# Reordering the steps of the first sweep in a two-sweep graph layer on one core

## The chip, the cores and the metric

One core of one Trainium2 chip runs the whole program. The metric is the device time of one execution in microseconds (us). Engines: PE is TensorE (PEld its weight loads), DVE is VectorE, ACT is ScalarE, POOL is GpSimd, SP is SyncE, which only issues transfers.

## The reference

64 samples of 256 tokens by 768 features. Per sample: layer norm and ReLU, then a graph layer with the adjacency matrix and its transpose, then a residual.

```python
h = jnp.maximum(_layernorm(x, axis=-1), 0.0)
ctx = jnp.matmul(adj, hs @ Wadj.T + badj) / deg_c[..., None]
ctx = ctx + jnp.matmul(radj, hs @ Wrev.T + brev) / rdeg_c[..., None]
ctx = ctx + hs @ Wself.T + bself
# ... plus two terms in the relations of the edges (rel), cut
x = x + ctx + rel
```

## The kernel before

Two sweeps over the samples: the first prepares features (three blocks per half: 0 and 1 in a tile `X`, 2 in a tile `Xs`), does some of the products and keeps `X` and `Xs` in HBM; the second loads them and does the rest. Nothing schedules the program but its own text: each engine runs its instructions in the order in which they are written. The text of a step is a list of items; primes say for how many samples ahead an item works (`xt''` in step t loads for sample t+2). Bare numbers such as `11a` or `2` are matrix products, with what ACT and DVE do for them. `d` holds four values per token (mean, scale and two degrees) in HBM, and `row` is the copy of it on every partition.

```python
for t in range(B):
    order = FIRST if t == 0 else SECOND if t == 1 else STEP1 if t + 1 < B else LAST1
    run(order, t, 1, PARTS1, PLACES1)
```

So STEP1 serves t = 2 to 62, 61 steps. The items that matter here:

```python
def store_left(b, n):                       # storeX, storeXs: issued on ACT
    ...
    nc.scalar.dma_start(s["kept_" + n], ...)          # X: 1536 KB, Xs: 768 KB

def spread(b):                              # spread
    nc.tensor.transpose(pt, v.rearrange("p c k -> p (c k)"), ident)   # one small transpose per step
    nc.scalar.activation(line, pt, AF.Copy)
    ...
        for c in range(C):                  # two pieces of 2 KB to HBM
            nc.sync.dma_start(d[:, c, :], line[c * 64 + NMEAN : c * 64 + RRDEG + 1, :])
        nc.sync.dma_start(                  # read back, one copy per partition: 512 KB
            s["row"].rearrange("p k i -> p (k i)"), d.rearrange("k c p -> (k c p)").partition_broadcast(P)
        )

# load_xt (xt): Xs <- x_t, 768 KB.  load_x (x): x, 768 KB.  load_sums (o0, o1), store_sums (out0, out1): 384 KB each.

def self_features(b, k):                    # self0, self1: on POOL, in place on Xs
    eng.tensor_tensor(v, v, row[:, k : k + 1, :].to_broadcast(...), op=(ALU.add, ALU.mult)[k])
def relu_features(b):                       # relu: on ACT
    nc.scalar.activation(S[b]["Xs"], S[b]["Xs"], AF.Relu)
def statistics(b, c):                       # on DVE, from x
    nc.vector.bn_stats(s["stats"][:, c, n, :], ...)
def aggregate(b, f):                        # u0 to u5: four matmuls into a bank pa (two of them), read by DVE
    ...
    nc.vector.tensor_mul(s["X"][:, f, :, :]..., pa, s["row"][:, 2:4, :]...)
```

## Time and profile before

| | us |
|---|---|
| timed executions, median of the first three | 2796.19 |
| the profiled execution, by itself | 2781.24 |
| its span | 2779.4 |
| of it: up to step 2 | 69.6 |
| steps 2 to 7 | 171.5 |
| steps 8 to 61 (54 steps) | 1389.4 |
| the rest, which is nearly all second sweep | 1148.9 |

A step is counted from one small transpose `pt` to the next. The main lines of this profile stand in the prediction below. POOL's order of time in one step (start, length, what): `self0'`, `a2+b2` and `self1'`. The first waits for the transposed x.

```profile
1101.80 3.52 POOL L534 TENSOR_TENSOR Xs<-Xs,row 128x1536 f32<-128x1536 f32 x1 [2.12 <-DMA Xs<-in_x_t_dram]
1105.27 1.85 POOL L562 TENSOR_TENSOR Xs<-Xs 128x768 f32<-128x768 f32 x1
1107.08 3.52 POOL L534 TENSOR_TENSOR Xs<-Xs,row 128x1536 f32<-128x1536 f32 x1
```

The transfer view of the stretch 1092.5 to 1094.4 us of the same step: per queue the packets, megabytes and share of the 16 engines. q10 is ACT's queue, q1 is SyncE's.

```profile
q10 hardware_dynamic: 112, 0.69, 88.6%
q1 hardware_dynamic: 8, 0.00, 0.5%
```

In these 1.9 us ACT's store of `Xs` has the engines nearly to itself. The 8 packets of SyncE's queue are the first piece of d and its completions; the second piece, issued at 1092.24, isn't among them.

### The profile page before, as it was taken

Reading aid. Unit: us, or ns where it says so; the run is one execution under the profiler, and the core shown is the slowest. Engines: PE = TensorE matmul, PEld = TensorE weight load, DVE = VectorE, ACT = ScalarE, POOL = GpSimd, SP = SyncE. Lnnn points to the kernel's source line nnn. Section 1 sums busy time; section 2 is a strip of 40 time slices with the busy share of each in tenths; the row PEclk is TensorE's granted clock in tenths of the full one; section 3 lists DMA queues with packets and bytes.
Section 4 is the critical chain, followed back from the end, with each engine's and each line's share of the span. In section 5 each row is a group of like instructions: output and inputs, shape, how many; then the busy total and the mean of one; then the engine's idle time right before and its main releaser. Section 6 shows DMA issues by size and latency. Waiting matters only on the chain.

```text
span 2779.4 us, 45451 instructions
## 1 busy us (share of the span) xinstructions
PE 2686.8 (97%) x16854; PEld 2472.1 (89%) x16854; DVE 2069.8 (74%) x3142; ACT 1757.2 (63%) x3099; POOL 1869.9 (67%) x1290
## 2 busy tenths in 40 slices
PE   5989999999999999999999998999999999999999
PEld 4779888888888898988898887899999999999998
DVE  7567776776777777777677775778888887887887
ACT  3557766766666766766676663566666656666665
POOL 5777777777777777777777775565565555555553
PEclk9999999999999999999999998999999999999999
DMA  7667777777777777777777777566666666766764
GB/s 251 250 222 262 260 256 254 256 260 258 255 262 252 263 263 258 266 255 262 252 259 260 260 249 253 211 243 252 256 243 247 257 247 241 259 245 241 258 248 162
DMA packets 237355, 695.46 MB, mean 250 GB/s; under 512 B 19388, under 2 KB 97716, under 8 KB 220744
## 3 DMA queue, kind: packets, MB, share of 16 engines
q1 hardware_dynamic: 200264, 390.49, 41.9%
q10 hardware_dynamic: 36864, 302.01, 27.4%
q8 instruction: 135, 2.21, 0.3%
q14 instruction: 92, 0.75, 0.1%
HBM read 436.05 MB, written 256.37 MB: 249 GB/s over the span
## 4 chain that ended last, share of the span: by engine, by line
PE 57%; DMA 15%; POOL 12%; DVE 7%; ACT 5%; issue 3%; SPq 1%; ACTq 0%; POOLq 0%; DVEq 0%
PE x L579 13%; DMA x<-in_x_dram 6%; POOL Xs L534 6%; DMA Xs<-in_x_t_dram 6%; PE y L579 5%; PE pa L545 4%; PE s L568 4%; PE z L579 4%; PE t L568 3%; PE u L568 3%; PE v L568 3%; PE x L568 3%; PE w L579 2%; PE s L579 2%; DMA d<-line 2%
## 5 line engine op out<-in xcount | busy, mean ns | idle before, releaser
L562 POOL TENSOR_TENSOR X<-X,Xs 128x768 f32<-128x768 f32 x256 | 475.9, 1881 | 464.5 <-DMA Xs<-kept_Xs 432.7
L534 POOL TENSOR_TENSOR Xs<-Xs,row 128x1536 f32<-128x1536 f32 (+1 forms) x128 | 446.8, 3491 | 215.7 <-DMA Xs<-in_x_t_dram 210.4
L294 ACT ACTIVATE top<-l 128x768 f32<-128x768 f32 x450 | 367.2, 816 | 219.4 <-DVE l L312 161.3
L312 DVE SCALAR_TENSOR_TENSOR l<-l,top 128x768 fp32r<-128x768 f32 x450 | 429.1, 954 | 15.4
L545 PE MATMUL pa<-a,hilo 128*128 128x512 f32 x1536 | 398.0, 400 | 37.3 <-DVE X L550 24.6
L545 PEld LDWEIGHTS pa<-a,hilo 128*128 128x128 f32 x1536 | 275.5, 189 | 101.6 <-DVE X L550 35.5
L579 PE MATMUL y<-w,X 128*128 128x256 f32 x1536 | 353.5, 380 | 0.0
L579 PEld LDWEIGHTS y<-w,X 128*128 128x128 f32 x1536 | 283.5, 190 | 34.4
L311 DVE TENSOR_TENSOR l<-X,top 128x768 fp32r<-128x768 f32 x285 | 269.9, 947 | 35.8 <-ACT top L294 35.1
L309 ACT ACTIVATE l<-X 128x768 fp32r<-128x768 f32 x285 | 238.0, 835 | 25.3 <-issue 19.1
L550 DVE TENSOR_TENSOR X<-pa,row 128x512 f32<-128x512 f32 x384 | 246.6, 681 | 9.0 <-PE pa L545 8.9
L423 DVE BATCH_NORM_STATS2 stats<-x 128x6 f32<-128x384 f32 x252 | 127.9, 549 | 149.9 <-DMA x<-in_x_dram 149.9
L562 POOL TENSOR_TENSOR a1+b<-X 128x768 f32<-128x768 f32 x64 | 118.1, 1845 | 155.1 <-PE w L579 154.4
L500 DVE SCALAR_TENSOR_TENSOR hilo<-x,cols,top_h 128x768 fp32r<-128x768 f32 x126 | 127.7, 1014 | 82.8 <-ACT top_h L294 82.8
L579 PE MATMUL x<-w,X 128*128 128x256 f32 x780 | 181.7, 383 | 1.2 <-issue 0.9
L579 PE MATMUL x<-w,Xs 128*128 128x256 f32 x768 | 176.2, 379 | 0.6 <-issue 0.6
L579 PE MATMUL w<-w,a1+b 128*128 128x256 f32 x768 | 176.4, 379 | 0.0
L579 PE MATMUL z<-w,Xs 128*128 128x256 f32 x768 | 176.1, 379 | 0.0
L579 PEld LDWEIGHTS x<-w,X 128*128 128x128 f32 x780 | 144.9, 192 | 19.0 <-issue 1.5
L579 PEld LDWEIGHTS x<-w,Xs 128*128 128x128 f32 x768 | 141.1, 190 | 18.0 <-issue 1.3
L579 PEld LDWEIGHTS z<-w,Xs 128*128 128x128 f32 x768 | 141.4, 190 | 16.8
L579 PEld LDWEIGHTS w<-w,a1+b 128*128 128x128 f32 x768 | 141.0, 190 | 16.7
(208 smaller groups left out, 6293.7 us busy)
## 6 DMA issues: line engine op xcount, KB each, us to landing
kept_X<-X ACTq DMA_DIRECT2D x64, 1536.0 KB
X<-kept_X ACTq DMA_DIRECT2D x64, 1536.0 KB
o<-in_x_dram SPq DMA_DIRECT2D x128, 384.0 KB
Xs<-in_x_t_dram SPq DMA_DIRECT2D x64, 768.0 KB
kept_Xs<-Xs ACTq DMA_DIRECT2D x64, 768.0 KB
sums<-o SPq DMA_DIRECT2D x128, 384.0 KB
o<-sums SPq DMA_DIRECT2D x128, 384.0 KB
Xs<-kept_Xs ACTq DMA_DIRECT2D x64, 768.0 KB
```

Of the source, the lines that this page charges most:

```text
L294: nc.scalar.activation(top.rearrange("p (f i) -> p f i", i=of.shape[-1]), of, AF.Copy)
L309: nc.scalar.activation(first, value, AF.Copy, scale=LOWER)
L311: nc.vector.tensor_tensor(others, value, top, op=ALU.subtract)
L312: nc.vector.scalar_tensor_tensor(diff, others.bitcast(F32), -STEP, top, op0=ALU.mult, op1=ALU.add)
L423: nc.vector.bn_stats(s["stats"][:, c, n, :], (s["o", c] if b == 0 else s["x"][:, c, :])[:, ts(n, HO)])
L500: nc.vector.scalar_tensor_tensor(hilo[:, 1, c, :], S[b]["x"][:, c, :], rstd, top, op0=ALU.mult, op1=ALU.subtract)
L534: eng.tensor_tensor(v, v, row[:, k : k + 1, :].to_broadcast([P, f1 - f0, L]), op=op)
L545: nc.tensor.matmul(pa, hilo[:, part, c, ts(f, P)], s["a"][:, c, :, :].rearrange("p s i -> p (s i)"), start=(k == 0), stop=(k == 2 * C - 1),)
L550: nc.vector.tensor_mul(s["X"][:, f, :, :].rearrange("p s i -> p (s i)"), pa, s["row"][:, 2:4, :].rearrange("p s i -> p (s i)"))
L562: (eng or nc.gpsimd).tensor_tensor(L[name], L[x], L[y], op=op)
L568: nc.tensor.matmul(bank, l[k][:, f, :], r[k][:, f, :], start=(k == 0 and f == 0), stop=(k == 1 and f == F - 1))
L579: nc.tensor.matmul(bank, l[:, f, :], r[:, f, :], start=(start and f == 0), stop=(row is None and f == F - 1), skip_group_check=not start,)
```

## The change

Its intent: STEP1 was ordered anew with a model of the transfers in which those in flight share the DMA engines equally. The same 52 items, permuted; nothing else.

```diff
 STEP1 = """
-self0' degrees0'' left' u4' u3' 5a statistics0'' 10a 5 u5' a2+b2 u0' self1' s11 statistics1'' degrees1'' 10
-u2' u1' s13 adj''' o1' 11a normal'' tokens'' 8 relu' 11 b0+b1' a0+a1+b0+b1 storeX' normalise1'' 2 s5' spread'' 3
-storeXs' normalise0'' a1+b1' xt'' second1'' b2-a1' second0'' 13a a1+b0+b1' x''' 14 13 s10' out1 out0 o0'
+left' a2+b2 u3' degrees0'' u4' 5a degrees1'' statistics0'' 10a adj''' self0' 5 u5' u0' s11 statistics1''
+self1' 10 u2' u1' s13 a0+a1+b0+b1 normal'' 11a tokens'' relu' 8 11 b0+b1' storeXs' normalise1'' storeX' o1'
+s5' 2 spread'' 3 normalise0'' second1'' second0'' 13a xt'' 14 x''' b2-a1' a1+b1' out1 13 a1+b0+b1' o0' out0
+s10'
 """
```

## The prediction

> **What bounds the kernel now.** I read the page first: the engines' shares, then the forty slices.
>
> ```profile
> PE 2686.8 (97%) x16854; PEld 2472.1 (89%) x16854; DVE 2069.8 (74%) x3142; ACT 1757.2 (63%) x3099; POOL 1869.9 (67%) x1290
> PE   5989999999999999999999998999999999999999
> DMA  7667777777777777777777777566666666766764
> ```
>
> TensorE (PE) is the bound; nothing else is near full. The second sweep begins near 1760 us. In the table by stretches its PE is busy 350.00 of 350 us (1850 to 2200) and 500.00 of 500 (2200 to 2700): nothing to gain there, and the change doesn't touch it. In the first sweep the same table has 296.15 of 300 (700 to 1000) and 292.68 of 300 (400 to 700). So all that this change can win is PE's idle time in the first sweep.
>
> Next, who waited for whom between 400 and 1600 us (about 47 steps; one step is one sample):
>
> ```profile
> POOL Xs L534 <- DMA Xs<-in_x_t_dram: 159.2, 47, 5.8
> DVE stats L423 <- DMA x<-in_x_dram: 120.9, 47, 4.7
> PEld pa L545 <- DVE X L550: 27.8, 35, 2.7
> PE pa L545 <- DVE X L550: 20.5, 27, 2.5
> ```
>
> PE's only wait of note is for a bank `pa` that VectorE (DVE) has not read yet; DVE was held before it by `statistics0''`, waiting for the load of x. GpSimd (POOL) waits longest, for the transposed x, but that has slack. A step with such a stall, on PE:
>
> ```profile
> 822.97 0.87 PE L579 MATMUL z<-w,l 128*128 128x256 f32 x6
> 825.38 2.13 PE L545 MATMUL pa<-a,hilo 128*128 128x512 f32 x8 [1.55 <-DVE X L550]
> ```
>
> I cut the sweep at the one small transpose per step (`pt`, L450) and measured 54 steps (about 241 to 1631 us). PE's own work is 25.08 us (1091.32 to 1116.40 is such a step, without a gap). The mean is 25.73, so 0.65 us of stall per step. All of it sits 15.94 us after `pt`, and its size follows one thing: when the statistics start. Up to 13.44 us after `pt` there is no stall, later each us costs a us (start 14.22: step 25.83; 15.31: 26.92; correlation 0.99). Mean start: 14.10. STEP1 is used for t = 2 to 62, 61 steps: 61 x 0.65 = **40 us, the most that the change can win**.
>
> Now why x comes late. The load queue of SyncE in that step without a gap:
>
> ```profile
> 1091.93 0.60 SPq L457 DMA_DIRECT2D d<-line  x2
> 1095.38 0.34 SPq L458 DMA_DIRECT2D row<-d  x1
> 1095.77 0.86 SPq L464 DMA_DIRECT2D kept_line<-line  x1
> 1096.73 0.38 SPq L389 DMA_DIRECT2D Xs<-in_x_t_dram  x1
> 1097.89 0.38 SPq L379 DMA_DIRECT2D x<-in_x_dram  x1
> 1098.33 1.75 SPq L402 DMA_DIRECT2D sums<-o  x2
> 1105.78 0.33 SPq L395 DMA_DIRECT2D o<-in_x_dram  x1
> ```
>
> `row` must wait until both 2 KB pieces of d have landed, 3.45 us after the first issue. By the packet records, the first piece moves 0.74 us after its issue, the second only 2.2 us after its own, just when the 768 KB of kept_Xs end. That store was issued on ScalarE (ACT) at the same moment:
>
> ```profile
> 1110.87 1.48 ACT L537 ACTIVATE Xs<-Xs 128x1536 f32<-128x1536 f32 x1
> 1112.01 0.33 ACTq L517 DMA_DIRECT2D kept_X<-X  x1
> 1117.01 0.31 ACT L462 ACTIVATE tokT<-line 128x128 fp32r<-128x128 f32 x1
> 1117.02 0.33 ACTq L517 DMA_DIRECT2D kept_Xs<-Xs  x1
> ```
>
> After that the SyncE queue runs as one train: row packets 1096.34 to 1098.79, transposed x to 1101.27, x after it. Over the 54 steps, row is issued 4.37 us after `pt` and the statistics start 9.73 us later (standard deviation 0.36). So **the issue of row sets the stall**.
>
> **What the Trainium skill says.** "DMA: Bandwidth & Descriptors", section Queues, rings and completion order: SP and ACT each have one ring on each of the 16 DMA engines, an engine takes descriptors of a ring in order and changes ring only after a whole packet of several descriptors. The trace agrees: kept_Xs gives each engine 8 descriptors (128 rows on 16), and the 2 KB piece sits behind all of them. In the second sweep, a 64 KB load issued at 2007.98, in the middle of the 1536 KB load of X (packets 2005.79 to 2010.67), moves its first packet at 2011.34. And within SyncE's ring, the 384 KB store issued 0.44 us behind the 768 KB load of x lets the next load go about 1.0 us after x arrives; with equal shares the half-sized one would be first. So the model behind this change, equal shares, isn't what this trace shows. The same page, section Issuing engines are not separate DMA queues, says that the starting engine gives no lane of its own: agrees. "Perfetto Trace Analysis", section Identifying the Most-Contended Engine, warns that matmul occupancy isn't distance from roofline; here it serves only to find gaps, and weight loads stand at 89%.
>
> **The change part by part.** The same 52 items, permuted; no instruction is added or removed. An engine runs its own items in order, so I compared the five orders.
>
> PE: u3' and u4' change places. Worth 0. SyncE: only o0' now goes before out0. o0' waits until out1 has landed (issue near 14.5 us after `pt`), so the 384 KB of out0 leave about 6.5 us later, behind x instead of close after it. Since it was behind x in the ring already: 0 to 0.1 us.
>
> POOL: a2+b2 (1.85 us) moves ahead of self0', into time in which POOL waits for the transposed x (2.12 us in the step shown); a0+a1+b0+b1 (1.83 us) moves ahead of normal''. From arrival to normal'' it was 3.52 + 1.85 + 3.52 = 8.9 us, it becomes 3.52 + 3.52 + 1.83 = 8.9 us. Worth 0; relu' could start 1.85 us earlier, but on ACT it stands behind 11a. DVE: s5' goes before 2, so it needn't wait for that product (2.0 us): b2-a1' comes some 1.5 us earlier, off the path. ACT: degrees1'' (1.8 us) moves between 5a and 10a; product 10 reads its bank near 15.1 us after `pt`, the scaling is then done by 13.7. Worth 0.
>
> The part that counts is ACT's stores: kept_Xs goes right behind relu', kept_X behind normalise1''. Counting from the next `pt`: relu' ends at -4.0 (1112.35 against 1116.40), kept_Xs is issued at -3.9, its packets start 0.85 later and take 2.1 (as they do now): -3.0 to -0.9. kept_X follows in the same ring, 3.9 to 4.3 us long as now: **-0.9 to about 3.0 to 3.4**. d is issued at about 0.6 as before and now meets the large store instead of the small one. It moves when that store has drained, about 3.0 to 3.4, and row goes out 0.64 us later, as now: 3.65 to 4.05, against a mean of 4.37. Gain on row, transposed x and x: 0.3 to 0.7, I take 0.45 us. Taking 0.45 off each of the 54 measured starts and keeping what lies above 13.44 leaves 0.33 us of stall instead of 0.68 on this measure: 0.35 x 61 = 21 us. Some of it I expect back from the stores' own scatter (kept_X lasts up to 5.2 us now), so I take 18: 2796 - 18 = **2778 us**.
>
> **The rivals.**
> 1. *Equal shares hold.* Then d slips past kept_X, row goes out near 2 us after `pt`, x is bound by its own issue (6.6), and the stall vanishes: 2796 - 40 = 2756. Against it: every one of the measured second pieces of d waited for the store's end.
> 2. *The large store holds d longer than the small one did.* Two stores back to back add their scatter; if kept_X drained at 4.3, row would go out at 4.95, 0.6 late: 1.26 - 0.68 = 0.59 us more per step, 36 us, 2832. For it: kept_X is twice as long, starts after its companion and depends on relu', hence on the transposed x. Against it: the sum above, which puts its end before the present one.
> 3. *A new wait.* a1+b0+b1' overwrites part of X and must wait for kept_X to land, now about 4 to 5 us after `pt`; POOL has until about 11 to start self0' and 3.7 us of work before it, so it should be absorbed. In the same way o1' now waits for out0 (about 18 us); it is needed a step later. About 2796 if this just eats the gain.
>
> **Range and chances.** 2756 needs the stall gone; 2800 is nothing gained. Runs before spread over 9 us. Range 2757 to 2806. Faster by 2% means 2740, below the floor of 2756: 0.01. Slower by 2% means 2852, 0.9 us more per step: 0.05. Rest 0.94.
>
> **What would show it.** Stall at the same place (pa after `pt`), smaller; statistics starting near 13.7 instead of 14.10; d's wait up to row shorter by some 0.4 us and both pieces of d moving when kept_X ends; POOL's wait for the transposed x about 2 us shorter per step through a2+b2 alone; second sweep unchanged. I am wrong if row goes out later than 4.4 after `pt`, or if PE shows a wait other than `pa`.

## The result

The changed kernel takes 2757.0 us (median of 4; 2749.22 to 2759.21) against 2797.48 us for the kernel before in the same rounds. The ratio is 0.9853, 95% interval 0.9822 to 0.9884. A ratio here is the mean time of one kernel's fast runs over that of the other's of the same rounds, so not quite the ratio of the two medians. The gain is 40 us. I had predicted 18, and the time lies on the lower edge of my range.

The page of the changed kernel: PE's, PEld's and the transfers' busy tenths.

```profile
PE   5989999999999999999999998899999999999999
PEld 4778999889899998989999997899999999999998
DMA  7676777777777777777777767576666666666764
```

Tenths are too coarse to show it; the table by stretches isn't. These are the lines of steps 8 to 61, first of the kernel before, then of the changed one (stretch, length, busy time of PE, PEld, DVE, ACT, POOL, then granted clock, DMA share and GB/s).

```profile
241.10:1630.50 1389.40, 1366.36 (x8048) 1233.01 (x8047) 1006.05 (x1674) 956.91 (x1782) 1060.90 (x811) 1.00 0.73 258
```

```profile
245.60:1607.00 1361.40, 1358.41 (x8048) 1232.52 (x8047) 1003.00 (x1675) 939.24 (x1783) 1068.59 (x810) 1.00 0.75 264
```

The same 8048 matmuls, and PE's idle time in this stretch falls from 23 to 3 us. (Busy time shrinks by 8 us too, in part because the record draws some matmuls behind a stall longer, as the 2.13 us for eight of them in the prediction's stall, where 2.02 is usual. The stretch itself is 28 us shorter; e1 below shows that this execution of the kernel before was a fast one.) The second sweep is the same: 350.00 of 350 and 500.00 of 500 us busy, as before.

Who waited for whom, 400 to 1600 us, in the changed kernel (total, times, longest):

```profile
POOL Xs L535 <- DMA Xs<-in_x_t_dram: 95.1, 48, 3.4
DVE stats L424 <- DMA x<-in_x_dram: 86.7, 48, 2.9
PEld pa L546 <- DVE X L551: 5.0, 10, 0.8
PE pa L546 <- DVE X L551: 2.8, 8, 0.6
```

PE's waits for a bank `pa` are down from 27.8 and 20.5 us to 5.0 and 2.8. They are the same waits at the same place, 15.95 us after `pt`, only rarer. The waits of POOL and DVE for loads shrink far less, and needn't: DVE has slack up to 13.44 us after `pt`.

ACT and SyncE in one step of the changed kernel (`pt` at 1455.94):

```profile
1450.41 1.48 ACT L538 ACTIVATE Xs<-Xs 128x1536 f32<-128x1536 f32 x1
1451.92 0.33 ACTq L518 DMA_DIRECT2D kept_Xs<-Xs  x1
1453.40 0.33 ACTq L518 DMA_DIRECT2D kept_X<-X  x1
```

```profile
1456.56 1.24 SPq L458 DMA_DIRECT2D d<-line  x2
1459.33 0.34 SPq L459 DMA_DIRECT2D row<-d  x1
1459.72 0.43 SPq L465 DMA_DIRECT2D kept_line<-line  x1
1460.24 0.38 SPq L390 DMA_DIRECT2D Xs<-in_x_t_dram  x1
1462.34 0.38 SPq L380 DMA_DIRECT2D x<-in_x_dram  x1
```

`kept_Xs` goes out right after the ReLU, `kept_X` 1.5 us later. By the packet records of this step, the packets of `kept_X` run from 1454.68 to 1458.53, and both pieces of d, issued at 1456.56 and later, move at 1458.38 to 1458.51. So d does wait until the store has all but drained, 1.8 us. That is still less than before, and row is issued 2.77 us after d instead of 3.45.

Means over steps 8 to 61, in us after `pt` unless said otherwise, with the standard deviation in brackets:

| | before | changed |
|---|---|---|
| kept_Xs issued | 0.85 | -4.02 (0.00) |
| kept_X issued | -4.34 | -2.45 (0.17) |
| last piece of d moves | 3.68 (0.36) | 2.74 (0.28) |
| row issued | 4.37 (0.39) | 3.60 (0.36) |
| transposed x has moved | 11.25 (0.77) | 10.37 (0.70) |
| statistics start | 14.10 (0.60) | 13.26 (0.54) |
| stall of PE per step | 0.65 | 0.13 |

### The profile page after: what moved, and what is told of

It is laid out like the page before. It is cut to its first block, busy times and chain, and to the rows that moved or that the text cites. A ratio compares the mean times of both kernels' runs of the same rounds, so it can differ in the third digit from the quotient of the medians.

```text
span 2757.4 us, 45566 instructions
## 1 busy us (share of the span) xinstructions
PE 2684.1 (97%) x16854; PEld 2476.0 (90%) x16854; DVE 2069.8 (75%) x3142; ACT 1737.5 (63%) x3099; POOL 1873.5 (68%) x1290
## 4 chain that ended last, share of the span: by engine, by line
PE 82%; DMA 7%; DVE 5%; POOL 3%; ACT 2%; issue 1%; SPq 0%; ACTq 0%; DVEq 0%; POOLq 0%
PE x L580 14%; PE y L580 11%; PE pa L546 10%; PE w L580 6%; PE z L580 6%; PE s L569 6%; DMA x<-in_x_dram 3%; PE t L569 3%; PE u L569 3%; PE v L569 3%; PE x L569 3%; PE s L580 3%; PE w L569 3%; PE z L569 2%; PE y L569 2%; PE v L580 2%
## 5 line engine op out<-in xcount | busy, mean ns | idle before, releaser
L563 POOL TENSOR_TENSOR b2-a<-Xs,X 128x768 f32<-128x768 f32 x64 | 118.9, 1857 | 185.3 <-DVE l L312 185.3
L312 DVE TENSOR_TENSOR l<-b0+b,top 128x768 fp32r<-128x768 f32 x62 | 59.2, 954 | 141.9 <-ACT top L295 141.9
```

Of the source, the lines that this page charges most:

```text
L312: nc.vector.tensor_tensor(others, value, top, op=ALU.subtract)
L563: (eng or nc.gpsimd).tensor_tensor(L[name], L[x], L[y], op=op)
```

## The experiments

**My theory** after the result: ACT's two stores alone decide, through d, row and x. **Rivals:** SyncE's exchange of `out0` and `o0'` (a store less beside x, which would matter with equal shares), and the moves on the other engines. Ratios are to the kernel before, in the same rounds on the same chip (e1 to e4 on one chip, e5 to e11 on another). Row, statistics and stall are means of steps 8 to 61 of one profiled execution each. All runs gave correct results.

| run | row issued | statistics start | stall per step | median us | ratio (95%) |
|---|---|---|---|---|---|
| e1, before again | 4.31 | 14.16 | 0.77 | 2795.85 | 0.9992 (0.9968 to 1.0015) |
| e2, stores only | 3.90 | 13.63 | 0.37 | 2770.5 | 0.9908 (0.9888 to 0.9928) |
| e3, all but stores | 4.41 | 14.08 | 0.71 | 2792.26 | 0.9979 (0.9958 to 1.0000) |
| e4, SyncE only | 4.41 | 14.11 | 0.75 | 2790.97 | 0.9975 (0.9951 to 0.9999) |
| e5, stores and POOL | 3.53 | 13.37 | 0.16 | 2760.28 | 0.9873 (0.9851 to 0.9895) |
| e6, transposed x ahead of row | 3.59 | 12.57 | 0.03 | 2754.91 | 0.9851 (0.9826 to 0.9876) |
| e7, kept_X ahead of relu' | 3.47 | 13.36 | 0.40 | 2773.3 | 0.9917 (0.9882 to 0.9953) |
| e8, kept_Xs late | 2.53 | 14.30 | 0.88 | 2801.76 | 1.0025 (0.9991 to 1.0058) |
| e9, both behind relu' | 3.30 | 13.19 | 0.16 | 2762.46 | 0.9867 (0.9835 to 0.9899) |
| e10, changed again | 3.61 | 13.43 | 0.22 | 2762.92 | 0.9878 (0.9854 to 0.9902) |
| e11, e6 again | 3.55 | 12.68 | 0.05 | 2754.92 | 0.9849 (0.9826 to 0.9873) |

### e1: the kernel before, once more

No edit.

> The kernel before, unchanged, profiled once more. My prediction took the stall (0.65 us per step, 40 us in all) from one execution of 2781 us, while the timed ones lie near 2797. Theory: the timed executions lose the missing 16 us to the same stall, so a profiled execution near 2797 shows about 56 / 61 = 0.9 us of stall per step, at the same place (the bank pa), the statistics starting near 14.35 us after pt, and the second sweep as long as before. Rival: the 16 us lie elsewhere (second sweep, clock, start), and the stall per step stays 0.65 at whatever time. Ratio to the kernel before 1.000 within 0.004 either way.

The profiled execution took 2797.01 us. Its line for steps 8 to 61:

```profile
252.10:1648.10 1396.00, 1369.27 (x8049) 1235.51 (x8048) 1006.86 (x1674) 957.46 (x1783) 1062.37 (x811) 1.00 0.73 257
```

So 0.77 us of stall per step, more than the 0.65 of the first record but less than the 0.9 expected. Against the first record, this stretch is 6.6 us longer, steps 2 to 7 are 8.2 us longer (179.7 against 171.5), the start 2.8 longer and the rest 1.9 shorter. The theory is half right: my base execution was a lucky one, some of its luck lay in the stall, and as much in the first steps. From this execution to the changed kernel's, 37.7 us go: 34.6 in steps 8 to 61, 4.7 in steps 2 to 7, 1.8 at the start, and 3.4 come back in the rest. Steps 2 to 7 take 171 to 180 us in all runs, whatever the order (171.5 in the first record, 171.0 in e2, 179.4 in e3, 171.1 in e10). The granted clock of that stretch goes along with it: 0.98 or 1.00 in the records with 171 to 172 us, 0.95 to 0.97 in all those with more. Which is cause and which effect isn't settled here.

### e2 and e3: the stores alone, and all but the stores

```diff
 # e2, on the kernel before
-... relu' 11 b0+b1' a0+a1+b0+b1 storeX' normalise1'' 2 s5' spread'' 3 storeXs' normalise0'' ...
+... relu' storeXs' 11 b0+b1' a0+a1+b0+b1 normalise1'' storeX' 2 s5' spread'' 3 normalise0'' ...
 # e3, on the changed kernel
-... b0+b1' storeXs' normalise1'' storeX' o1' s5' 2 spread'' 3 normalise0'' ...
+... b0+b1' storeX' normalise1'' o1' s5' 2 spread'' 3 storeXs' normalise0'' ...
```

> The kernel before with nothing changed but the two stores of ScalarE: kept_Xs right behind relu', kept_X behind normalise1''. Theory (the stores hold up d, d holds up row, row holds up x): row is issued near 3.6 us after pt instead of 4.37, statistics start near 13.3, stall near 0.13 us per step, ratio 0.985 to 0.988, so the whole gain. Rival 1 (the gain comes from SyncE's exchange of out0 and o0', which takes a store out from behind x): ratio 0.995 to 1.000 and the statistics near 14. Rival 2 (ScalarE's, VectorE's and GpSimd's other moves): the same, 0.995 to 1.000.

> The changed kernel with the two stores of ScalarE put back where the kernel before has them. Theory: the gain is gone, ratio 0.996 to 1.002, row issued near 4.3 us after pt, stall 0.6 us per step or more. Rivals 1 and 2: ratio near 0.985 to 0.990, because the exchange on SyncE and all other moves are kept.

e3 came out as the theory has it: without the stores' move hardly anything is left (0.9979). But e2 missed the 0.985 to 0.988 that I expected: it brings only 26 of 40 us, so the stores alone aren't the whole. Two parts that give 26 and 6 us apart give 40 together: something else helps the stores. The table of e2 shows where: `kept_Xs` is issued at -3.65 us with a scatter of 0.35, in the changed kernel at -4.02 with none. The view of the tile Xs in e2 (241 to 1600 us; idle us, times) says what held up the instructions that use it; the second line is the ReLU waiting for POOL (a third, 2.3 us for the adjacency load, is left out).

```profile
  DMA Xs<-in_x_t_dram: 156.0, 53
  POOL Xs L534: 13.9, 25
```

### e4: SyncE's exchange alone

```diff
-... s10' out1 out0 o0'
+... s10' out1 o0' out0
```

> The kernel before with only o0' and out0 exchanged on SyncE. Theory: x is ahead of out0 in the same ring anyway, so statistics start no earlier than 14.0 us after pt, ratio 0.997 to 1.002. Rival 1 (equal shares between transfers in flight, so 384 KB less beside x): x arrives up to 1 us earlier, the statistics start near 13.4, ratio 0.985 to 0.990.

The statistics start 14.11 us after `pt`, 9.70 after row's issue; in the two records of the kernel before it was 9.73 and 9.85. So x isn't faster with one store less behind it, and rival 1 falls. The ratio of 0.9975 lies within the 0.997 to 1.002 that the theory expected, and its interval nearly touches 1; steps 8 to 61 are as long as e1's within 1.3 us (1394.7). If there are 7 us in it, they aren't in the stall that this study is about. That is left open.

### e5: the stores and POOL's exchange

```diff
 # on e2
-self0' degrees0'' left' u4' u3' ... 5 u5' a2+b2 u0' self1' ... 11a normal'' ... b0+b1' a0+a1+b0+b1 normalise1'' ...
+left' a2+b2 self0' degrees0'' u4' u3' ... 5 u5' u0' self1' ... 11a a0+a1+b0+b1 normal'' ... b0+b1' normalise1'' ...
```

> The kernel before with the stores moved as in e2 and, on GpSimd, a2+b2 ahead of self0' and a0+a1+b0+b1 ahead of normal''. e2 alone gave 0.991, because kept_Xs went out at -3.65 us before pt with a scatter of 0.35, while in the changed kernel it goes out at -4.02 with none. Theory: relu' (and so kept_Xs) waits for self1', which the transposed x holds up; with a2+b2 out from between self0' and self1' that wait is gone. Then kept_Xs is issued at -4.0 with a scatter under 0.1, row near 3.6, stall near 0.15 us per step, ratio 0.984 to 0.987: the whole gain of the change. Rival: GpSimd's exchange is worth nothing, as I predicted (the chain up to normal'' has the same length), and the rest of the gain comes from the other moves: ratio near 0.991, kept_Xs at -3.65 as in e2.

`kept_Xs` is issued at -4.02 with no scatter, the stall is 0.16 and the time 2760.28 us. The same view of the tile Xs as for e2 has one line left:

```profile
  DMA Xs<-in_x_t_dram: 42.8, 43
```

The ReLU never waits for POOL now: `a2+b2` is out from between `self0'` and `self1'`, so when the transposed x comes late, `self1'` ends 1.85 us sooner. The ratios of e2 and e5 alone would be thin evidence, since their intervals just overlap; the scatter of `kept_Xs` and the view above carry the argument. GpSimd's two exchanges weren't tried apart. Together with the stores they are the change, as far as can be measured. The others (PE's, DVE's, ACT's degrees, SyncE's, and on GpSimd `b2-a1'` going before `a1+b1'`) account for what is between 0.9873 and the 0.9853 and 0.9878 of the changed kernel, which is nothing that can be told from noise.

### e8: the small store out of d's way, but late

```diff
 # on the kernel before
-... spread'' 3 storeXs' normalise0'' a1+b1' xt'' second1'' b2-a1' second0'' 13a ...
+... spread'' 3 normalise0'' a1+b1' xt'' second1'' b2-a1' second0'' storeXs' 13a ...
```

> The kernel before with kept_Xs moved late instead of early: behind second0'', when d and row are long issued. Theory (the second piece of d is held by kept_Xs alone): both pieces move 0.75 us after their issues, row is issued near 2.4 us after pt instead of 4.3. But kept_Xs then moves beside the transposed x and x, 768 KB or 1.9 us at 400 GB/s, so the statistics start between 12.4 and 14.2 us after pt and the ratio lies between 0.98 and 1.00. Rival (d is slow by itself, not because of the store): row stays near 4.3.

SyncE in one step:

```profile
1054.35 0.61 SPq L457 DMA_DIRECT2D d<-line  x2
1055.94 0.34 SPq L458 DMA_DIRECT2D row<-d  x1
1056.33 0.43 SPq L464 DMA_DIRECT2D kept_line<-line  x1
1056.87 0.38 SPq L389 DMA_DIRECT2D Xs<-in_x_t_dram  x1
```

row follows d by 1.59 us instead of 3.45, on average it is issued at 2.53: the store was what made d wait longer than this. Yet the kernel isn't faster: the statistics (14.30) and the ratio (1.0025) lie just outside what I expected. `kept_Xs`, issued at 4.77, now moves from 8.17 to 11.96 on average, among the packets of the transposed x and x. Row is 1.8 us earlier than in e1, and the statistics start 0.1 later. The whole gain at one end of the train is lost in its middle.

### e7 and e9: does the order of the two stores matter?

```diff
 # both on the changed kernel
-... tokens'' relu' 8 11 b0+b1' storeXs' normalise1'' storeX' o1' ...
+... tokens'' storeX' relu' storeXs' 8 11 b0+b1' normalise1'' o1' ...       # e7
+... tokens'' relu' storeX' storeXs' 8 11 b0+b1' normalise1'' o1' ...       # e9
```

> The changed kernel with kept_X issued ahead of relu' and kept_Xs behind it: both stores early, in the other order. Theory (d waits until ScalarE's ring is drained, whatever is last in it): the ring drains at the same time or up to 0.3 us earlier, row at 3.2 to 3.7 us after pt, ratio 0.984 to 0.987 as for the changed kernel. Rival (it matters that the small store is out of the way and the large one last): row near 4.3 and ratio near 0.995.

> The changed kernel with both stores right behind relu', the large one first: relu' storeX' storeXs'. It does properly what e7 set out to do: e7 held relu' behind the large store's wait, so line and d came 1.0 us late (d issued at 1.62 us after pt). Theory (d waits until all of ScalarE's ring is drained; the order within it doesn't matter): kept_X goes out near -4.4, kept_Xs near -4.0, the ring drains near 2.4, d moves then, now behind kept_Xs packets of 6144 bytes, row is issued at 3.0 to 3.4 us after pt (3.41 median in the changed kernel), stall 0.15 us per step or less, ratio 0.982 to 0.987. Rival (what helps is that the small store is away from d, and with it last the wait of the kernel before is back): row near 4.2, ratio 0.993 or more.

e7 was badly built, and its ratio is a miss: ahead of the ReLU, the large store's wait for its data held up the ReLU and all behind it on ACT, so `kept_Xs` went out at -2.57 and d at 1.62 (0.78 in the changed kernel). Row was early all the same (3.47), and the rival's 4.3 wasn't seen; of the stall of 0.40, two steps of 28.8 and 29.9 us make 0.16. e9 asks the same question properly. The last packet of its stores starts at 2.61 on average and ends at 2.88, the last piece of d moves at 2.48 and row is issued at 3.30. The ratio, 0.9867, is that of the changed kernel. So it doesn't matter which store is last; it matters when ACT's ring is nearly empty.

### e6, e10 and e11: a version with the train closed up

In the changed kernel SyncE still sits and waits for d with nothing moving behind it. The transposed x needs nothing of d.

```diff
 # on the changed kernel, in spread(b, with_xt)
     for c in range(C):
         nc.sync.dma_start(d[:, c, :], line[c * 64 + NMEAN : c * 64 + RRDEG + 1, :])
+    if with_xt:
+        load_xt(b)
     nc.sync.dma_start(s["row"]..., d...partition_broadcast(P))
 # STEP1
-s5' 2 spread'' 3 normalise0'' second1'' second0'' 13a xt'' 14 ...
+s5' 2 spreadxt'' 3 normalise0'' second1'' second0'' 13a 14 ...      # spreadxt: spread(b, True)
```

> The changed kernel, but SyncE issues the transposed x between the two pieces of d and row, so it doesn't wait for d to land with nothing behind it. Theory: SyncE's ring is one train, x comes when all before it has moved; the train starts when kept_X has drained (about 2.5 us after pt) instead of 1.2 us later with row, so the statistics start near 12.0 to 12.4 us after pt instead of 13.26, the stall goes from 0.13 to about 0.01 us per step, and the time to 2757 - 8 = about 2749, ratio 0.982 to 0.984. Rival: row now comes behind 768 KB, lands near 9 us or later, and the banks pa of u3' (read near 10.2) or self0' wait for it: ratio 0.986 or more with a wait on row.

> The changed kernel, unchanged, timed and profiled once more beside e11 on the same chip. Ratio 0.983 to 0.988, row near 3.6 us after pt (mean), stall 0.1 to 0.2 us per step.

> The kernel of e6 again, beside the changed kernel on the same chip. Theory: it takes away what stall is left in steps 8 to 61 (0.13 us per step, 7 us in all), so it is 4 to 8 us faster than e10: ratio to the kernel before 0.002 to 0.003 below e10's. Rival: nothing is left to win there, both ratios agree within 0.001.

SyncE in one step of e6:

```profile
1051.13 1.24 SPq L458 DMA_DIRECT2D d<-line  x2
1052.47 0.69 SPq L390 DMA_DIRECT2D Xs<-in_x_t_dram  x1
1053.91 0.34 SPq L461 DMA_DIRECT2D row<-d  x1
```

The statistics start at 12.57 us, a little later than I expected, and the stall is 0.03 us per step. The rival's late row does show, as POOL waiting for it (22.9 us in e11 from 400 to 1600 us), but it doesn't reach PE. e6's 2754.91 us missed the 2749 that I had expected. I had taken 8 us off the changed kernel's 2757, which is itself from one set of rounds; so I ran both side by side, and there the changed kernel's median is 2762.92. Steps 8 to 61 of e10 (the changed kernel) and of e11:

```profile
246.00:1612.10 1366.10, 1359.07 (x8048) 1231.26 (x8046) 1001.48 (x1674) 939.30 (x1784) 1067.87 (x810) 1.00 0.75 263
```

```profile
244.80:1602.00 1357.20, 1355.62 (x8048) 1230.37 (x8047) 1007.67 (x1674) 937.54 (x1782) 1070.26 (x810) 1.00 0.77 265
```

The stretch is 8.9 us shorter, and the medians differ by 8.0 us (2762.92 against 2754.92). The mean of e11's runs over that of e10's is 0.997. It beats both kernels, by little: 54 steps without any stall would be 54 x 25.08 = 1354.3 us, so 3 us are left in this stretch. (e10's stall, 0.22, is a little above what I expected of it.)

## Why the prediction was wrong

**What held.** PE's stall in the first sweep is nearly all that there is to win; it sits at the bank `pa`; it follows the start of the statistics (in the changed kernel 14.32 us gives a step of 25.94, 14.00 one of 25.62, anything below 13.4 gives 25.08). d waits for ACT's store to drain, and x follows row at a fixed distance, 9.73 us before and 9.66 after. SyncE's, PE's, DVE's moves and that of degrees1'' are worth nothing that can be seen in the stall. (One exchange was overlooked: on GpSimd `b2-a1'` also goes before `a1+b1'` and starts at 1.46 us after `pt` instead of 4.75. e5 does without it.) Rival 2 (the large store holds d longer) and rival 3 (a new wait) did not come. POOL's wait for `kept_X` is 0.7 us in total, from 400 to 1600 us. Rival 1 named about the measured time, but not its reason: d didn't slip past the store, it waited almost until its end. Of the signs, POOL's wait for the transposed x fell by 1.4 us per step (3.4 to 2.0), not by 2.

**What failed.** The step that put the number off is the second below: the mechanism was right, but the gain on row was put at 0.45 us and measured 0.77. Stall down from 0.65 to 0.13 us per step is 61 x 0.52 = 32 us, where I had counted 21 and then taken 3 off. The third, the base, adds to it. The first was a wrong reading that hid in the sum, which took `kept_Xs` at -3.9 from a step without a stall; the changed kernel has -4.02, the stores alone -3.65.

1. "Worth 0; relu' could start 1.85 us earlier, but on ACT it stands behind 11a." I compared the chains up to normal'', which are equally long, and looked at the ReLU in a step without a stall, where 11a is indeed last. In many others POOL is last. The waits of the kernel before, 400 to 1600 us, of which the prediction shows four lines, had it:

```profile
ACT Xs L537 <- POOL Xs L534: 18.3, 28, 1.1
```

Over the 54 steps its ReLU ends 3.62 us before `pt` on average (scatter 0.39), not 4.0. In the kernel before this cost nothing, because the store of `Xs` was issued 4.5 us later anyway; once the store follows the ReLU, it counts. e2 against e5: 0.9908 against 0.9873, stall 0.37 against 0.16.

2. "Gain on row, transposed x and x: 0.3 to 0.7, I take 0.45 us", and the 3 us that I took off for scatter. Row came 0.77 us earlier and the statistics 0.84. I let `kept_X` drain "-0.9 to about 3.0 to 3.4"; its packets start at -1.23 on average and the last ends at 3.12, so the store was placed well. But d doesn't wait for that last packet: its last piece moves at 2.74 on average and at 2.55 in the median. The kernel before has the same lead: there the last piece moves at 3.68 and the store's last packet ends at 4.05, 0.37 us later. I had taken the two for one ("just when the 768 KB of kept_Xs end"). Presumably the engines that carry d are done before the others; the packet records don't name the engine. No scatter came back; that of the statistics fell from 0.60 to 0.54. With 0.8 instead of 0.45, the same rule on the same 54 starts gives 0.18 us of stall, close to the 0.13 measured (0.22 in e10). So the rule was right and its input was not.

3. "2796 - 18". The stall was read from an execution of 2781 us and taken off a median of 2796. e1's execution, at 2797, has 0.77 us per step instead of 0.65, which is 6.6 us in 54 steps, and 8.2 us more in steps 2 to 7. With e1's stall, "the most that the change can win" would have been 61 x 0.77 = 47 us. How much of it the fastest run of the changed kernel (2749.22) has won isn't known: it wasn't profiled. e11, with 0.05 us of stall left, has a median of 2754.92, so the floor of 2756 wasn't far off.

As to equal shares: the trace refutes that for these transfers. The new order puts both pieces of d behind 1536 KB, and they wait for nearly all of it. That the order is good nevertheless is because the stores as a whole end earlier (3.12 us after `pt` on average instead of 4.05). What the model made of it can't be seen here.

## What to carry to other kernels

Where a small transfer heads a chain (here 2 KB that release 2 MB of loads), ask what is in flight on the other ring at that moment, and count it as waiting for nearly all of that, as d did here; then see that big stores are issued as soon as their data is ready, and that what makes the data isn't held up by other work on its engine. Don't move such a store to where it merely misses the small transfer, for it may land among the loads that follow (e8). And judge a part on the slow steps, not on a clean one, and take a kernel's stall and its base time from the same execution.

## What the Trainium skill lacked or had wrong

- "DMA: Bandwidth & Descriptors", section Queues, rings and completion order, says that an engine switches between rings only after a whole packet of several descriptors. The runs agree, but the page gives no time for it: a 2 KB transfer that moves 0.74 us after its issue on idle engines moved 2.2 us after it behind a store of 768 KB, and 1.8 us behind the second half of one of 1536 KB. Taking that store away (e8) let row be issued at 2.53 instead of 4.31 us.
- The same section has the rings served in turn. With two transfers waiting in ACT's ring that isn't plain here: in the second sweep, a 64 KB load on SyncE, issued at 2007.98, did not move when ACT's load of X had ended (2010.67), but between 2011.34 and 2013.90, over the time of the next one in ACT's ring (2009.97 to 2013.82). No run here settles why.
- No page that I read says how much the stalls of one kernel differ between executions: for the kernel before 0.65 and 0.77 us per step here, and 171.5 and 179.7 us for steps 2 to 7.
